# Sums of squares of attention keys in a four-stage fused kernel: one column of ones per block against a row of 512 per head, two heads side by side

## The chip, the cores and the metric

The kernel runs on one core of a Trainium2 chip. The core has TensorE (PE in the profile; PEld is its weight load), VectorE (DVE), ScalarE (ACT), GpSimd (POOL) and SyncE (SP, which here issues most DMAs), an SBUF of 128 partitions, and PSUM, to which TensorE writes. Each engine takes its instructions in the order in which the program gives them. The metric is device time in microseconds (us) of one launch, the median of several runs; lower is better.

## The reference

Four layers on x of 4 batches by 512 tokens by 512 channels, with a context of 4 by 512 by 256: a selective scan over the context, gated by the normed x; a mixture of 64 experts with 8 of them for each token; cross attention with 16 heads of 128; and a feed-forward with values rounded to integers. The change touches the third alone:

```python
def rmsnorm(x, g, eps=EPS):
    var = jnp.mean(jnp.square(x), axis=-1, keepdims=True)
    return x * jax.lax.rsqrt(var + eps) * g
...
q = (hidden_states @ Wq).reshape(B, Sq, H, D)
k = (encoder_hidden_states @ Wk).reshape(B, Skv, H, D)
v = (encoder_hidden_states @ Wv).reshape(B, Skv, H, D)
q = rmsnorm(q, gq)
k = rmsnorm(k, gk)
scores = jnp.einsum('bqhd,bkhd->bhqk', q, k) * scale
attn = jax.nn.softmax(scores, axis=-1)
out = jnp.einsum('bhqk,bkhd->bqhd', attn, v)
out = out.reshape(B, Sq, H * D)
return out @ Wo
...
x = x + _L0_xattn_ref(ctx_1024, _layernorm(x, axis=-1), ...)
x = x + _L0_ffn_ref(_layernorm(x, axis=-1), ...)
x = x + _L1_xattn_ref(_layernorm(x, axis=-1), ctx_1024, ...)
x = x + _L1_ffn_ref(_layernorm(x, axis=-1), ...)
```

There are 4 x 16 = 64 pairs of a batch and a head; each has 512 keys of 128 values, and for each key the sum of the squares of its 128 values is wanted.

## The kernel before

Keys depend on the context only, not on the layers before the attention. So the kernel makes them ahead of time, spread as small tasks through the earlier stages, and keeps them in DRAM until the attention reads them. Times below are from the start of the profiled span.

**The keys' tasks.** The class Keys (lines 1194 to 1258) has four steps for one pair of a batch and a head, and every stage calls them where it has room:

- task (line 1223): TensorE multiplies the 128 weight columns of the head by the context, four instructions into a PSUM bank pk of 128 (values of a key) by 512 (keys).
- evict: ACT writes two copies from PSUM to SBUF: k_sq, the squares (line 1232), and k_kT, the keys times gk (line 1233). SP sends k_kT, 256 KB, to DRAM (k_dram, line 1234).
- squares (line 1243): the sums over the 128 partitions. Each block of 128 columns of k_sq is the weight of a matmul with one column of ones; the result is one column of a PSUM tile kpss of 128 by 4. A float32 matmul is two instructions in the profile, so a head has 8.
- take (line 1255): ACT divides by 128 and adds the epsilon into k_ms, 128 by 4, and SP writes it to four columns of ms_dram (line 1257).

k_sq is free again when TensorE has read it. Which SBUF tile it lives in is asked of the stage (row), as is the PSUM bank (psum).

**Where they run.** 64 heads are split so: in the scan 5 each of batches 1, 2 and 3, and all 16 of batch 0 in its last quarter; in the route 17; in the attention the last 16, heads 8 to 15 of batches 2 and 3 (KEYS_LATE).

- The scan (0 to about 509) works through 128 steps q; in each, POOL multiplies dBu (line 494), ACT makes dA by exponentials, VectorE scans and TensorE turns the products. A plan gives each head its q: task at the end of step q, evict at the start of q+2, squares at its end, take at the start of q+3. The heads of batches 1 to 3 start at steps 14, 22, 24, 26 and 30 of a batch's 32, those of batch 0 at every second step.
- The route (to about 635) chooses each token's experts. A loop over 16 blocks of 128 tokens, two in a turn, normalises (g_xn), turns (g_pt), multiplies by the gate (g_plT), takes exponentials and masks (g_z, stored in z_dram; POOL presets the tile by memsets). From its second turn on it makes one head in each turn, with squares and take of the head of the turn before between the next blocks' turns and the logits. After the loop a plan by due times places the steps: mapping, ranks and codes, then lists of tokens (ol, ob, ot and the product plist). A helper two_keys gives the task of one head, then squares and take of the head before, then the eviction of the new one. It is placed twice ahead of the lists and once at the end, and four more heads lie among the lists.
- The experts (to about 1293): 64 in order, each with gathers by POOL, turns of the gathered rows (pt, line 1307, copied by ACT or VectorE to xT), pg (line 1343), and po (lines 1367, 1377). Small tasks are placed between the experts, as many per expert as the count of tasks demands. The last are key_norms (lines 1605 to 1626): load the means of squares of 48 heads from ms_dram as 128 by 192, take the inverse square roots (ACT's root, then VectorE), and then turn them by TensorE in two steps (kpt, krows), so that each row has 128 keys, and store the rows in r_dram, from which the attention reads rows broadcast over partitions.
- The attention (to the end) starts with 8 of the late heads, one every 2.6 us of its plan (some_keys: task, squares of the head before, evict, take of the head before), while POOL gathers the experts' results (yg) and adds them up. Then four windows of 14.5 us of plan each project the queries (pq) of a block of tokens, with two key heads in each. k_sq is a tile of the ring of two called planes, k_kT one of the ring of seven called oT; planes is afterwards filled by the attention's own transposes by DMA. The means of squares go directly into columns of an SBUF tile ms. last_norms (line 2346) takes the inverse roots in unit 16 of the steady loop, and last_keys (line 2349) turns and stores them in unit 24.

Of the kernel before, what the change touches and what calls it, by code (L numbers as in the profile page):

```python
# [17 lines left out]
F32 = mybir.dt.float32  # L18
# [12 lines left out]
P = 128  # L31
# [4 lines left out]
EPS = 1e-5  # L36
# [206 lines left out]
def ssm_phase(ctx, cm, x_all, w, kv, router_stats):  # L243
# [347 lines left out]
    def ahead_ends(b, s):  # L591
# [11 lines left out]
        if s == 23:  # L603
# [6 lines left out]
    keys = Keys(cm, w, kv, cm.k_small, lambda n: pool[1].tile([P, S], F32, name=f"k_{n}"),  # L610
                lambda shape, name: ps.tile(shape, F32, name=name, tag=banks[name]),
                lambda b: (st[b]["ctx"], 0))
# [5 lines left out]
    def key_task(b, h, bank):  # L618
        banks.update(pk=bank, kpss="pv")
        keys.task(b, h)  # L620
# [119 lines left out]
def moe_phase(ctx, cm, x_all, w, kv, dr, router_stats, out):  # L740
# [20 lines left out]
    with ExitStack() as es:  # L761
# [3 lines left out]
        keys = Keys(cm, w, kv, cm.k_small, None, None, None)  # L765
# [29 lines left out]
def route(ctx, cm, x_all, w, dr, router_stats, r, more, late, keys, ex):  # L795
# [91 lines left out]
    def key_row(n):  # L887
        if n == "sq":
            return cp.tile([P, S], F32, name="k_sq")
# [300 lines left out]
    plan.run()  # L1190
    assert not left


class Keys:
# [6 lines left out]
    def __init__(self, cm, w, kv, small, row, psum, ctx, direct=None):  # L1201


        self.cm, self.nc, self.w, self.kv = cm, cm.nc, w, kv
        self.small, self.row, self.psum, self.ctx, self.direct = small, row, psum, ctx, direct
        self.wk = {}
        self.pk = self.sq = self.pss = None
# [19 lines left out]
    def evict(self):  # L1227
# [3 lines left out]
        sq, kT = self.row("sq"), self.row("kT")  # L1231
# [3 lines left out]
        self.pk, self.sq = None, (b * H + h, sq)  # L1235

    def squares(self):
        if self.sq is None:
            return
        i, sq = self.sq  # L1240
        pss = self.psum([P, self.KB], "kpss")
        for j in range(self.KB):
            self.nc.tensor.matmul(pss[:, j:j + 1], sq[:, j * P:(j + 1) * P], self.cm.ones[:, 0:1],  # L1243
                                  start=True, stop=True)
        self.sq, self.pss = None, (i, pss)

    def take(self):
        if self.pss is None:
            return
        i, pss = self.pss  # L1250
        if self.direct is None:
            ms = self.small.tile([P, self.KB], F32, name="k_ms")
        else:
            ms, self.direct = self.direct[:, 0:self.KB], self.direct[:, self.KB:]
        self.nc.scalar.activation(ms, pss, AF.Copy, bias=EPS, scale=1.0 / HD)
        if self.direct is None:
            self.nc.sync.dma_start(self.kv["ms"][:, i * self.KB:(i + 1) * self.KB], ms)
# [218 lines left out]

def slot_tasks(cm, dr, kv, r, pool, ps):
# [119 lines left out]
    cols = []  # L1597
    for k in range(B * H + 1):
        if k < B * H and k not in late:
            if not cols or cols[-1][1] < k * KB:  # L1600
# [952 lines left out]
```

## The time and the profile before

| | us |
|---|---|
| median of 3 runs | 2471.33 |
| lowest, highest run | 2467.07, 2478.49 |
| the profiled execution, its own time | 2469.94 |
| its span in the trace | 2468.2 |

The mean TensorE clock of the profiled execution was 0.979 of full. The groups of the instructions that the change touches:

| group | count | busy us | mean ns of one |
|---|---|---|---|
| PE kpss (line 1243), 128x1 out | 512 | 66.8 | 251 |
| PEld kpss, 128x128 weights | 512 | 65.1 | 196 |
| ACT k_ms from kpss, 128x4 | 64 | 10.8 | 169 |
| ms_dram from k_ms, issue by SP, 2.0 KB each | 48 | | 320 |
| k_dram from k_kT, 256.0 KB each | 64 | | |

A group's busy time counts overlapping instructions once, its mean is the time of one as it was recorded; matmuls are pipelined, so what a series takes on TensorE is read from where the next one starts. In a timeline each line has start, duration, engine, line, operation, output and inputs, shapes and count; a bracket at its end says how long the engine was idle before it and what ended that. In a chain each piece is what the next one waited for. A row of stretches has for each engine its busy time in a stretch of the span, and then the granted clock, the busy share of the DMA engines and GB/s.

### The profile page before, as it was taken

What the parts mean: (1) busy time and instruction counts of PE and PEld (TensorE: products, weight loads), DVE (VectorE), ACT (ScalarE), POOL (GpSimd) and SP (SyncE); (2) the same over time, 40 slices, a digit from 0 to 9 for tenths busy, and PEclk for the clock granted to TensorE, in tenths of its full rate; (3) what the DMA queues carried; (4) which work ended last, traced back from release to release, by engine and by line L of the source; (5) the groups of instructions that cost most, each with busy time, mean ns of one, the idle gap of its engine ahead of it and who ended that gap; (6) DMA issues with size and microseconds to landing.
All of it is one profiled execution on the core that took longest, in us unless ns stands there. A gap on an engine that the chain in (4) does not pass through costs nothing. (4 is left out here: it accounts for less than half of the span.)

```text
span 2468.2 us, 29177 instructions
## 1 busy us (share of the span) xinstructions
PE 2330.2 (94%) x8819; PEld 1268.0 (51%) x8819; DVE 1590.2 (64%) x2872; ACT 1414.0 (57%) x2647; POOL 1332.1 (54%) x1314
## 2 busy tenths in 40 slices
PE   5989899988899999999998999999999999999998
PEld 2555555655555656666664444444444444444444
DVE  6999998956244434444324477667776778666655
ACT  6777777755333333344433466667666666667654
POOL 7999999940444434544426356356644655333323
PEclk8999998998999999999998999999999999999999
DMA  5362727343689868899976478678866887566530
GB/s 213 94 231 90 246 86 246 103 163 110 211 254 294 265 226 276 272 285 346 303 220 214 152 190 219 155 186 196 188 160 159 190 191 175 136 156 150 132 78 26
DMA packets 479892, 468.01 MB, mean 190 GB/s; under 512 B 313247, under 2 KB 354287, under 8 KB 475632
## 3 DMA queue, kind: packets, MB, share of 16 engines
q1 hardware_dynamic: 434686, 305.77, 46.3%
q0 software_dynamic: 42992, 160.13, 20.0%
q8 instruction: 72, 1.18, 0.2%
q14 instruction: 92, 0.75, 0.1%
q10 hardware_dynamic: 2050, 0.18, 0.1%
HBM read 316.11 MB, written 79.82 MB: 160 GB/s over the span
## 5 line engine op out<-in xcount | busy, mean ns | idle before, releaser
L1343 PE MATMUL pg<-xT,wg 128*128 128x284 f32 (+12 forms) x1536 | 389.4, 399 | 2.3 <-ACT xT L1310 1.3
L2027 POOL COPY planes<-e 128x512 int16<-128x512 int16 x174 | 119.2, 685 | 397.5 <-DVE e L2008 215.5
L1999 DVE TENSOR_REDUCE mx<-psc 128x1 f32<-128x512 f32 x256 | 176.3, 689 | 243.0 <-PE psc L1996 240.2
L1343 PEld LDWEIGHTS pg<-xT,wg 128*128 128x128 f32 x1536 | 280.4, 191 | 93.1 <-issue 40.2
L494 POOL TENSOR_TENSOR dBu<-bb,du 128x1024 f32<-128x1024 f32 x128 | 304.8, 2411 | 6.6 <-DVE dA L519 5.5
L2002 ACT ACTIVATE e<-psc,mx 128x512 f32<-128x512 f32 x256 | 176.3, 689 | 148.6 <-DVE mx L1999 77.6
L1996 PE MATMUL psc<-kT,qT 128*128 128x512 f32 x512 | 260.0, 594 | 0.0
L2068 PE MATMUL po<-eT,v 128*128 128x512 f32 x512 | 236.8, 605 | 13.5 <-ACT eT L2062 10.7
L1264 POOL DMA_INDIRECT xg<-xn_dram,tok x168 | 176.4, 1050 | 123.9 <-PE pt L1307 59.9
L1962 PE MATMUL pq<-Wq,xnT 128*128 128x512 f32 x512 | 231.8, 595 | 4.8 <-ACT xnT L1918 3.9
L2077 PE MATMUL px<-Wo,oT 128*128 128x512 f32 x512 | 231.2, 595 | 2.3 <-DVE qn L1980 2.3
L505 ACT ACTIVATE dA<-delta,negA 128x512 f32<-128x512 f32 x256 | 176.3, 694 | 50.9 <-DVE hc L520 37.3
L519 DVE TENSOR_TENSOR_SCAN dA<-dA,dBu 128x1024 f32<-128x1024 f32 x80 | 185.7, 2322 | 15.2 <-ACT dA L505 7.9
L1264 POOL DMA_INDIRECT wd<-down,widx x64 | 61.9, 967 | 225.1 <-PE po L1377 212.0
L2068 PEld LDWEIGHTS po<-eT,v 128*128 128x128 f32 x512 | 92.0, 189 | 150.7 <-issue 91.8
L1962 PEld LDWEIGHTS pq<-Wq,xnT 128*128 128x128 f32 x512 | 96.2, 190 | 129.8 <-issue 110.6
L2077 PEld LDWEIGHTS px<-Wo,oT 128*128 128x128 f32 x512 | 95.1, 190 | 125.5 <-issue 105.5
L525 PEld LDWEIGHTS yT<-ident,hc 128*128 128x128 f32 x1024 | 118.6, 143 | 74.5 <-issue 42.4
L1883 POOL DMA_INDIRECT yg<-y_dram,pos x108 | 118.1, 1094 | 59.0 <-issue 50.1
L1388 ACT COPY yo<-po 128x512 f32<-128x512 f32 (+3 forms) x64 | 37.5, 586 | 195.3 <-PE po L1377 150.5
L525 PE MATMUL yT<-ident,hc 128*128 128x128 f32 x1024 | 132.0, 276 | 17.6 <-DVE x_all L560 9.9
L1388 DVE COPY yo<-po 128x512 f32<-128x512 f32 x68 | 46.9, 691 | 151.3 <-PE po L1377 151.3
(380 smaller groups left out, 4696.6 us busy)
## 6 DMA issues: line engine op xcount, KB each, us to landing
y_dram<-yo SPq DMA_DIRECT2D x110, 256.0 KB
bb<-bc_dram SPq DMA_DIRECT2D x16, 1024.0 KB
cb<-bc_dram SPq DMA_DIRECT2D x16, 1024.0 KB
v_dram<-v SPq DMA_DIRECT2D x64, 256.0 KB
k_dram<-k_kT SPq DMA_DIRECT2D x64, 256.0 KB
kT<-k_dram SPq DMA_DIRECT2D x64, 256.0 KB
rk<-r_dram SPq DMA_DIRECT2D x64, 256.0 KB
v<-v_dram SPq DMA_DIRECT2D x64, 256.0 KB
```

Of the source, the lines that this page charges most:

```text
L494: nc.gpsimd.tensor_tensor(dBus[q], st[b]["bb"][i // 2][:, j:j + 2, :], st[b]["du"][c].unsqueeze(1).to_broadcast([P, 2, S]), ALU.mult)
L505: nc.scalar.activation(dAs[q][:, j, :], st[b]["delta"][c], AF.Exp, scale=negA[:, c, n:n + 1])
L519: nc.vector.tensor_tensor_scan(*flat, 0.0, ALU.mult, ALU.add)
L525: nc.tensor.matmul(yT[:, lc, :], t[:, lc * P:(lc + 1) * P], cm.ident, is_transpose=True, start=first and lc == 0, stop=last, skip_group_ch ...
L1264: nc.gpsimd.indirect_dma_start(out=t[0:n, :], out_offset=None, in_=table, in_offset=bass.IndirectOffsetOnAxis(ap=index, axis=0))
L1343: nc.tensor.matmul(pg[:, 0:n], s["wg"][:, c, m * P:(m + 1) * P], s["xT"][:, c, 0:n], start=c == 0, stop=c == NC - 1)
L1962: nc.tensor.matmul(pq.rearrange("p h d -> p (h d)"), xnTs[b * NC + i][:, c, :], s["Wq"][:, c, :], start=c == 0, stop=c == NC - 1)
L1996: nc.tensor.matmul(pscore, st[b, g]["qT"][:, h, i * P:(i + 1) * P], ks[n], start=True, stop=True)
L1999: nc.vector.tensor_reduce(mx, pscore, AX.X, ALU.max, negate=True)
L2002: nc.scalar.activation(e, pscore, AF.Exp, bias=mx, accum_out=tot)
L2068: nc.tensor.matmul(po, v[:, kc, :], eT[:, kc, :], start=kc == 0, stop=kc == KB - 1)
L2077: nc.tensor.matmul(px, oTs[j * HG + h][:, i * P:(i + 1) * P], st[b, g]["Wo"][:, h, :], start=h == 0, stop=h == HG - 1)
```

## The change

The sums of squares come out as a row. The weights are now 64 columns of ones, and the moving operand is the whole k_sq of 512 columns, so that a head is one matmul (two instructions) whose 64 output rows are all the same sum. Two heads go one after the other, the first into the PSUM partitions 0 to 63, the second into 64 to 127. squares does nothing until two heads have been evicted (n=2), but the heads of batches 1 to 3 in the scan go alone (n=1), and a last head that is left over can be forced (last=True), which the end of the route does.

take makes one copy from PSUM of 128 (or 64) by 512, in place over the k_sq of the first head of the pair, and one DMA of a 2 KB row for each head into ms_dram, which is now 64 by 512. A k_sq tile is therefore held until that row has left. The tiles of a pair: in the scan's last quarter two pairs in the former taps tile; in the route one tile with two halves; in the attention two tiles of the ring oT, from which k_kT is taken as well, in place of planes.

With rows in DRAM the norms need no turn: any layout of 128 partitions will do for the inverse root, so they are loaded flat, and stored flat (move_norms). key_norms has three steps instead of four. The late heads of the attention go through ms_dram as well, and the three steps of last_norms (load, root, store) are in the units 16, 20 and 24.

```diff
@@ -607,15 +607,29 @@
 
 
     banks = {}
-    keys = Keys(cm, w, kv, cm.k_small, lambda n: pool[1].tile([P, S], F32, name=f"k_{n}"),
+    spare = []
+
+    def key_row(n):
+        if n == "kT" or keys.n == 1:
+            t = pool[1].tile([P, S], F32, name=f"k_{n}")
+            return t if n == "kT" else [t]
+        if not spare:
+            t = cp.tile([P, NC, DC, P], F32, name="k_sqs", tag="taps")
+            spare.extend([t[:, i].rearrange("p j s -> p (j s)") for i in range(k, k + 2)]
+                         for k in (0, 2))
+        spare.append(spare.pop(0))
+        return list(spare[-1])
+
+    keys = Keys(cm, w, kv, key_row,
                 lambda shape, name: ps.tile(shape, F32, name=name, tag=banks[name]),
-                lambda b: (st[b]["ctx"], 0))
+                lambda b: (st[b]["ctx"], 0), n=1)
     key_plan = {}
 
     def key_at(q, ends, f, *a):
         key_plan.setdefault((q, ends), []).append((f, a))
 
     def key_task(b, h, bank):
+        keys.n = 1 if b > 0 else 2
         banks.update(pk=bank, kpss="pv")
         keys.task(b, h)
 
@@ -762,7 +776,7 @@
         more = es.enter_context(tc.tile_pool(name="b_more", bufs=1))
         r["tok"] = more.tile([P, 3, E], I32, name="tok")
         r["widx"] = more.tile([P, E], I32, name="widx")
-        keys = Keys(cm, w, kv, cm.k_small, None, None, None)
+        keys = Keys(cm, w, kv, None, None, None)
         with tc.tile_pool(name="e_w", bufs=4) as wp:
             ex = Experts(cm, w, dr, y_dram, r, wp)
             route(cm, x_all, w, dr, router_stats, r, more, late, keys, ex)
@@ -886,7 +900,8 @@
 
     def key_row(n):
         if n == "sq":
-            return cp.tile([P, S], F32, name="k_sq")
+            t = cp.tile([P, 2, S], F32, name="k_sq")
+            return [t[:, 0], t[:, 1]]
         if not kTs:
             t = late.tile([P, 2, S], F32, name="k_kT", tag="hq")
             kTs.extend([t[:, 0], t[:, 1]])
@@ -1188,6 +1203,8 @@
     for f in (some_key, keys.evict, two_keys, key_ends):
         plan.at(U + 1.8 * NT + 5, f)
     plan.run()
+    keys.squares(last=True)
+    keys.take()
     assert not left
 
 
@@ -1198,13 +1215,16 @@
     KC = CTX // P
     KB = S // P
 
-    def __init__(self, cm, w, kv, small, row, psum, ctx, direct=None):
+    HALF = P // 2
+
+    def __init__(self, cm, w, kv, row, psum, ctx, n=2):
 
 
         self.cm, self.nc, self.w, self.kv = cm, cm.nc, w, kv
-        self.small, self.row, self.psum, self.ctx, self.direct = small, row, psum, ctx, direct
+        self.row, self.psum, self.ctx, self.n = row, psum, ctx, n
         self.wk = {}
-        self.pk = self.sq = self.pss = None
+        self.pk = self.pss = None
+        self.sqs, self.free = [], []
 
     def load(self, h0, h1, pool, tag, queue=None):
 
@@ -1228,33 +1248,35 @@
         if self.pk is None:
             return
         b, h, pk = self.pk
-        sq, kT = self.row("sq"), self.row("kT")
+        if not self.free:
+            self.free = self.row("sq")
+        sq, kT = self.free.pop(0), self.row("kT")
         self.nc.scalar.activation(sq, pk, AF.Square)
         self.nc.scalar.activation(kT, pk, AF.Copy, scale=self.cm.gkq)
         self.nc.sync.dma_start(self.kv["k"][b, h], kT)
-        self.pk, self.sq = None, (b * H + h, sq)
-
-    def squares(self):
-        if self.sq is None:
+        self.pk = None
+        self.sqs.append((b * H + h, sq))
+
+    def squares(self, last=False):
+
+        if len(self.sqs) < self.n and not (last and self.sqs):
             return
-        i, sq = self.sq
-        pss = self.psum([P, self.KB], "kpss")
-        for j in range(self.KB):
-            self.nc.tensor.matmul(pss[:, j:j + 1], sq[:, j * P:(j + 1) * P], self.cm.ones[:, 0:1],
-                                  start=True, stop=True)
-        self.sq, self.pss = None, (i, pss)
+        pss = self.psum([P, S], "kpss")
+        for j, (_, sq) in enumerate(self.sqs):
+            self.nc.tensor.matmul(pss[j * self.HALF:(j + 1) * self.HALF, :],
+                                  self.cm.ones[:, 0:self.HALF], sq, start=True, stop=True)
+        self.pss, self.sqs, self.free = (self.sqs, pss), [], []
 
     def take(self):
         if self.pss is None:
             return
-        i, pss = self.pss
-        if self.direct is None:
-            ms = self.small.tile([P, self.KB], F32, name="k_ms")
-        else:
-            ms, self.direct = self.direct[:, 0:self.KB], self.direct[:, self.KB:]
-        self.nc.scalar.activation(ms, pss, AF.Copy, bias=EPS, scale=1.0 / HD)
-        if self.direct is None:
-            self.nc.sync.dma_start(self.kv["ms"][:, i * self.KB:(i + 1) * self.KB], ms)
+        sqs, pss = self.pss
+        ms = sqs[0][1]
+        at = slice(0, len(sqs) * self.HALF)
+        self.nc.scalar.activation(ms[at], pss[at], AF.Copy, bias=EPS, scale=1.0 / HD)
+        for j, (i, _) in enumerate(sqs):
+            self.nc.sync.dma_start(self.kv["ms"][i:i + 1, :],
+                                   ms[j * self.HALF:j * self.HALF + 1, :])
         self.pss = None
 
 
@@ -1474,6 +1496,18 @@
     return ctx
 
 
+def move_norms(nc, kv, rk, runs, load):
+
+    KB, at = S // P, 0
+    for k0, k1 in runs:
+        flat = (kv["ms"][k0:k1, :].rearrange("k s -> (k s)") if load else
+                kv["r"][k0 * KB:k1 * KB, :].rearrange("n p -> (n p)"))
+        flat = flat.rearrange("(p m) -> p m", p=P)
+        part = rk[:, at:at + (k1 - k0) * KB]
+        nc.sync.dma_start(*((part, flat) if load else (flat, part)))
+        at += (k1 - k0) * KB
+
+
 def slot_tasks(cm, dr, kv, r, pool, ps):
 
 
@@ -1594,43 +1628,27 @@
 
     KB = S // P
     late = {b * H + h for b, h in KEYS_LATE}
-    cols = []
-    for k in range(B * H + 1):
-        if k < B * H and k not in late:
-            if not cols or cols[-1][1] < k * KB:
-                cols.append([k * KB, k * KB])
-            cols[-1][1] += KB
-    n = sum(c1 - c0 for c0, c1 in cols)
+    runs = []
+    for k in range(B * H):
+        if k not in late:
+            if not runs or runs[-1][1] < k:
+                runs.append([k, k])
+            runs[-1][1] += 1
+    n = sum(k1 - k0 for k0, k1 in runs) * KB
 
     def key_norms(step):
         if step == 0:
             c["rk"] = pool.tile([P, n], F32, name="krk")
-            at = 0
-            for c0, c1 in cols:
-                nc.sync.dma_start(c["rk"][:, at:at + c1 - c0], kv["ms"][:, c0:c1])
-                at += c1 - c0
         elif step == 1:
             rsqrt(nc, pool, c["rk"], c["rk"], "k")
             return lambda: None
-        else:
-            a0, a1 = (step - 2) * P, min((step - 1) * P, n)
-            pt = ps.tile([P, P], F32, name="kpt", tag="pt")
-            pe.transpose(pt[0:a1 - a0, :], c["rk"][:, a0:a1], cm.ident)
-            rows = pool.tile([P, P], F32, name="krows")
-            act.copy(rows[0:a1 - a0, :], pt[0:a1 - a0, :])
-            at = 0
-            for c0, c1 in cols:
-                lo, hi = max(at, a0), min(at + c1 - c0, a1)
-                if lo < hi:
-                    nc.sync.dma_start(kv["r"][c0 + lo - at:c0 + hi - at, :],
-                                      rows[lo - a0:hi - a0, :])
-                at += c1 - c0
+        move_norms(nc, kv, c["rk"], runs, step == 0)
 
     calls = [(load,), (rooms,), (many,), (row, "limit"), (row, "first"), (weigh, 0), (weigh, 1)]
     calls += [(inside, n) for n in range(4)] + [(tops, q) for q in range(NT // NC)]
     calls += [(remap, q) for q in range(NT // NC)]
     calls += [(weight, k, i) for k in range(TOPK) for i in range(3)] + [(finish,)]
-    norms = [(key_norms, i) for i in range(2 + -(-n // P))]
+    norms = [(key_norms, i) for i in range(3)]
     return [[lambda f=f, a=a: f(*a) for f, *a in part] for part in (calls, norms)]
 
 
@@ -2260,11 +2278,16 @@
 
     n_ms = len(KEYS_LATE) * KB
     ms = pool[1].tile([P, n_ms], F32, name="k_ms")
+    late_runs = []
+    for b, h in KEYS_LATE:
+        if not late_runs or late_runs[-1][1] < b * H + h:
+            late_runs.append([b * H + h, b * H + h])
+        late_runs[-1][1] += 1
 
     def key_row(n):
 
         if n == "sq":
-            return pool[2].tile([P, S], F32, name="k_sq", tag="planes")
+            return [pool[7].tile([P, S], F32, name="k_sq", tag="oT") for _ in range(2)]
         return pool[7].tile([P, S], F32, name=f"k_{n}", tag="oT")
 
     def key_bank(shape, name):
@@ -2272,10 +2295,8 @@
             return pav.tile(shape, F32, name=name, tag="po")
         return psc.tile(shape, F32, name=name, tag="psc")
 
-    keys = Keys(cm, w, kv, small, key_row, key_bank,
-                lambda b: (ctx_k[b], 0), direct=ms)
+    keys = Keys(cm, w, kv, key_row, key_bank, lambda b: (ctx_k[b], 0))
     keys.wk = wk_k
-    first = KEYS_LATE[0][1]
 
     steps = []
 
@@ -2343,18 +2364,11 @@
     for n in range(3):
         later(FRONT + (0, 2.5, 3.2)[n] * WINDOW + 9, norm_k, n, nc.vector)
 
-    def last_norms():
-        rsqrt(nc, small, ms, ms, "late")
-
-    def last_keys():
-        pr = ptr.tile([n_ms, P], F32, name="pkr", tag="pt")
-        nc.tensor.transpose(pr, ms, cm.ident)
-        rows = pool[1].tile([n_ms, P], F32, name="k_rows", tag="xn_d")
-        nc.scalar.copy(rows, pr)
-        for b in (2, 3):
-            at = (b * H + first) * KB
-            nc.sync.dma_start(kv["r"][at:at + n_ms // 2, :],
-                              rows[(b - 2) * n_ms // 2:(b - 1) * n_ms // 2, :])
+    def last_norms(step):
+        if step == 1:
+            rsqrt(nc, small, ms, ms, "late")
+        else:
+            move_norms(nc, kv, ms, late_runs, step == 0)
 
 
     for *_, f, a in sorted(steps, key=lambda x: x[:2]):
@@ -2363,8 +2377,8 @@
     load_q(2)
     load_o(0, 0)
     load_kv(3)
-    put(back, KB * 3 + 4, last_norms)
-    put(back, KB * 5 + 4, last_keys)
+    for step in range(3):
+        put(back, KB * (3 + step) + 4, last_norms, step)
 
 
     for u in range(KB, len(heads) * KB + 2):
@@ -2484,7 +2498,7 @@
     dp = ctx.enter_context(tc.tile_pool(name="kv", bufs=1, space=DRAM))
     kv = dict(v=dp.tile([B, H // HG, P, S // P, HG * HD], F32, name="v_dram"),
               k=dp.tile([B, H, HD, S], F32, name="k_dram"),
-              ms=dp.tile([P, B * H * (S // P)], F32, name="ms_dram"),
+              ms=dp.tile([B * H, S], F32, name="ms_dram"),
               r=dp.tile([B * H * (S // P), P], F32, name="r_dram"))
     dr = dict(xn=dp.tile([B * S, DM], F32, name="xn_dram"),
               z=dp.tile([NT, P, 3, Gate.W], F32, name="z_dram"))
```

## The prediction

> **What bounds the kernel now.** I read the page first (engines, slices, chain), then the stretches stage by stage, then the timeline around each place where squares of keys are made, and last the chain through the start of the attention.
>
> The page: TensorE is busy 94% of the span, and the chain that ended last names its lines first. The squares (L1243) stand there with 0%, which is a share of the whole span only.
>
> ```profile
> PE 2330.2 (94%) x8819; PEld 1268.0 (51%) x8819; DVE 1590.2 (64%) x2872; ACT 1414.0 (57%) x2647; POOL 1332.1 (54%) x1314
> PE po L2068 8%; PE pq L1962 7%; PE psc L1996 6%; PE px L2077 6%; PE pf L2181 2%; DMA turned<-planes 2%; PE ph L2146 1%; DVE mx L1999 1%; PE pk L1223 1%; PE pet L2061 1%; ACT e L2002 1%; ACT Th L2111 1%; DVE e L2008 0%; PE kpss L1243 0%; DVE x_all L1891 0%
> ```
>
> Stretches (start:end, length, then busy us of PE, PEld, DVE, ACT, POOL, clock, DMA share): the scan (85 to 505) has PE, DVE and POOL all above 90%, POOL highest; the route (505 to 640) has no full engine, so its time is latency from one engine to the next; the experts (700 to 1276) are TensorE's, 571 of 576.
>
> ```profile
> 85.00:200.00 115.00, 104.61 (x462) 61.67 (x461) 109.60 (x79) 86.39 (x141) 110.14 (x57) 0.97 0.51 167
> 505.00:580.00 75.00, 63.44 (x319) 38.00 (x317) 36.23 (x178) 42.92 (x94) 20.91 (x80) 0.93 0.43 149
> 580.00:640.00 60.00, 49.10 (x290) 32.71 (x286) 33.77 (x75) 29.45 (x46) 12.06 (x12) 0.84 0.36 117
> 700.00:1276.00 576.00, 571.06 (x2548) 369.36 (x2545) 245.43 (x473) 219.22 (x465) 261.85 (x257) 1.00 0.90 281
> ```
>
> Timeline of the route: the squares stand between a wait for ACT and the logits, on TensorE's path; two heads later an f16 copy (ot) follows k_sq and k_kT on ACT, and VectorE waits for what it feeds.
>
> ```profile
> 545.72 1.05 PE L1243 MATMUL kpss<-ones,k_sq 128*128 128x1 f32 x8 [0.40 <-ACT k_kT L1233]
> 546.70 1.94 PE L204 MATMUL g_plT<-g_xT,gwT 128*64 128x256 f32 x8
> ...
> 556.28 0.10 POOL L221 MEMSET g_z<- 128x4 f32 x1 [0.46 <-DMA z_dram<-g_z]
> ...
> 590.93 0.17 ACT L1255 ACTIVATE k_ms<-kpss 128x4 f32<-128x4 f32 x1 [1.26 <-PE kpss L1243]
> 591.00 0.59 ACT L1232 ACTIVATE k_sq<-pk 128x512 f32<-128x512 f32 x1
> 592.05 1.16 ACT L1033 ACTIVATE ot<-ol,tok 128x1024 f16<-128x1024 f16 x1
> 594.65 0.96 DVE L1026 TENSOR_TENSOR ob<-slot_col,col 128x1536 f16<-128x1536 int16 x1 [2.86 <-PE plist L1041]
> 635.38 1.07 PE L1307 MATMUL pt<-ident,xg 128*128 128x128 f32 x8
> ```
>
> Chain through the attention's start (start, us, what): key projections and squares alternate and end in the first pq; later two squares stand between pq's.
>
> ```profile
> 1310.85 2.55 PE kpss L1243 x8
> 1318.01 1.87 PE kpss L1243 x8
> 1333.23 3.45 PE pq L1962 x8
> 1375.24 0.79 PE kpss L1243 x8
> 1390.21 0.79 PE kpss L1243 x8
> ```
>
> **Prices.** One head before: 8 instructions, 0.79 us in the chain when warm. One head as a row of 512 is one f32 matmul, two instructions; px, pq and pk in the chain take 0.43 per instruction (pq x8 3.45), so 0.86. A pair is 0.86 if its two column halves run together and 1.72 if one after the other. The nearest row is the expert's pair of half-array matmuls (po L1377, 64-row tiles): four instructions occupy TensorE from 1206.80 to 1207.86, 1.06. I take 1.1 a pair against 1.58 for two heads before. ACT's k_ms was 0.17; a 128x512 copy from PSUM is 0.59 (yo L1388, v L482), so +0.42 a take, +0.25 a pair.
>
> The new wait: squares' tile is written in place by the take and is free only when its row has landed in DRAM; before, TensorE's read freed it. Price of one return: semaphore records give 1.4 us after issue for the ms store of 626.89 and 5.9 for that of 635.75, behind other transfers; the z store, issued at 553.13, released POOL at 555.68, 2.5. I take 2 in the quiet route, 3.4 in the attention's start (DMA share 0.74 in 1310 to 1360); 1.4 and 5.9 are the bounds.
>
> The Trainium skill, TensorEngine Tiling (Array Packing), Key Properties, says that changing the tiling mode drains TensorE, which speaks against the change: every pair is set between full-array matmuls. The 1.06 above has both switches in it and is 0.2 over one full matmul of 0.86; were a drain as long as a whole matmul, the pair would be 1.72 and the sum some 6 us higher. No column pair is in this trace.
>
> **Step by step.**
>
> 1. Scan, 31 heads. 15 alone: TensorE +0.07 each, +1.0; 16 as 8 pairs: 8 × (1.1 − 1.58) = −3.8. ACT: 23 × 0.59 − 31 × 0.17 = +8.3. ACT is busy 86 of 115 us and POOL 110, so this hides under dBu and hc on POOL; without that cover +8.3 at most, −3.8 at best. For the heads of batches 1 to 3 the single sq tile is refilled one step (450 us for 128 dBu, 3.5) after the take; behind a late square on ACT stands dA, for which VectorE's scan waits, with buffers between. Taken: 0. But the last pair has no cover: the cast of ident and g_xn queue behind its take (508.53, g_xn 508.80): +0.42 on ACT and +0.3 on TensorE (1.1 − 0.79), **+0.7** (0 to 1.4).
>
> 2. Route loop. Seven heads had their squares in six turns of 7.0 us and once behind the loop (0.98 start to next, after a wait of 0.40). Now three turns have a pair and three none; nothing is left behind the loop. In a turn without, g_plT may start when g_pt ends (545.33) rather than at 546.70: 1.37. But the exps (549.91, 556.92) also wait for POOL's memset, that for the z store of the turn before: exps 549.91 to memset's end 556.34 is 6.43, so a turn gets no shorter than that and gains 0.58. Three × −0.58, behind the loop −0.98, pairs +0.1 each; the longer take falls into ACT's 0.5 us wait for g_plT. **−2.4**; −5.1 if z doesn't hold (3 × 1.37 + 0.98), +0.7 with serial halves and takes on the path.
>
> 3. Two heads ahead of the lists (586 to 594). The second head's k_sq needs the pair's tile: squares 589.95 + 1.1, take to 591.7, store back at 593.7 by the 2 us, k_sq; ot follows 1.05 later at 594.75 instead of 592.05: **+2.7**, since VectorE and TensorE wait for ot's plist already (2.86). With 1.4: +2.1; with 5.9: +6.6. The same wait at 575 to 583 falls into an ACT that idles 6.96 us ahead of 588.49: nothing; if that cover were gone, as here. Token lists: two longer takes, +0.42 each, one of which plist waits for: **+0.5** (0 to 1).
>
> 4. Route's end. Seventeen heads are odd: pair 14/15 is squared, taken (632.76 + 1.1 + 0.6), stored; head 16's k_sq waits, is squared alone, and only behind that, in TensorE's order, stands the first expert's pt. Store back at 636.5, k_sq 0.6, squares 0.9: pt at 638 instead of 635.38, +2.6. The copy behind pt started only at 638.47, by a wait that the trace leaves unnamed, so part is slack: **+2.0** (0.2 with all of it slack, 6.6 with a return of 5.9). The experts, full on TensorE, keep this shift.
>
> 5. Norms among the experts. Two turns by TensorE (0.44 in all) go, and ACT's second krows copy with its 5.39 us wait for the r store; that expert's turn took 9.05 against 8.4 to 8.5 of its neighbours. **−0.9** (0 to −1). Loads and stores stay three or four, with flat rows; their queue is full either way. The square root stays.
>
> 6. Attention's start, TensorE then POOL. On the chain to pq at 1333.23 the squares are 8.9 us (0.79, 0.79, 2.55, 1.87, 1.03, 0.79, 1.05); four pairs at 1.1 to 2.2 (half clock) save about 4. Against it: kT of heads 3, 5 and 7 takes a slot of the ring of seven that an in-place row leaves one turn (2.6) earlier; issue 0.3 + 3.4 − 2.6 = 1.1, three times 3.3. **−0.7**; −4 with quick returns, 3 × (0.3 + 5.9 − 2.6) − 4 = +6.8 with slow ones. POOL, idle 10.4 us ahead of qms, passes it on.
>
> 7. Windows to 1400: the squares at 1375.24 and 1390.21 leave the chain, the pairs go to 1382 and 1397, where TensorE waits 0.5 for qn: **−1.6** (−1.6 to 0). The late norms: eight more pairs of row stores, loads and stores at three places, the turn of 0.27 and the copy of 0.26 gone, all long before the first use: 0.
>
> Sum: 0.7 − 2.4 + 2.7 + 0.5 + 2.0 − 0.9 − 0.7 − 1.6 = +0.3. The profiled execution took 2469.94 us (span 2468.2, 1.7 around it), 1.4 under the median of the runs; +0.3 on the median 2471.33 gives 2471.6, rounded to 2472.
>
> **Rivals.**
> - Rows come back late (slower). One mechanism: the in-place tile held until its store lands, at three places on the path. At 5.9: 6.6 + 6.6 + 6.8 with the other terms unchanged (0.7 − 2.4 + 0.5 − 0.9 − 1.6 = −3.7) is +16.3: 2488. It decides over 0.5% from about 5.2 on. For it: the store of 635.75, in the very place. Against: that of 626.89.
> - Gains without givebacks (faster). Returns of 1.4 and z not binding: 0.4 − 5.1 + 2.1 + 0 + 0.2 − 0.9 − 4 − 1.6 = −8.9: 2462. For it: TensorE is the chain at the attention's start. Against: POOL gathers yg from 1340 on without a break, so 4 us of that may hide.
> - The halves don't overlap: each pair 1.72, +0.6 at some ten pairs on the path: +6, 2478. For it: none is in the trace to deny it. Against: 1.06 for two row tiles.
> - The scan loses its cover, ACT's 8.3 showing whole: 2480. Against: ACT's 25% idle.
>
> **How the numbers follow.** Forecast 0.45, late rows 0.22, faster 0.18, serial halves 0.08, scan 0.07. About 0.5%, 12.4 us, is what a measurement of this kernel tells from no change: 2459 to 2484. Late rows mostly pass 2484, the others seldom; of the faster case a good half passes 2459 only if TensorE's relief also reaches the scan's −3.8. So faster 0.15, same 0.58, slower 0.27. The range takes both neighbours in: 2459 to 2488.
>
> **What would show it.** Squares: four instructions a pair, ending within 1.1. Route turns alternating near 6.4 and 7.1. ACT waiting for an ms store ahead of k_sq near 592 and 635; the first ot near 594.7; the first pt near 638. The r wait of 5.4 gone. pq's first at about the same distance from the attention's start. The forecast is wrong if pairs take 1.7, if stalls name the ms store for over 5 us each, or if the stretches up to 505 change length at all.

## The result, and the profile after

The changed kernel takes 2481.2 us (median of 22 runs, 2468.09 to 2492.32); the kernel before, in the same comparison, 2470.24 (22 runs, 2460.98 to 2485.11). The ratio is 1.0046, with a 95% interval of 1.0033 to 1.0059: 11 us slower. The profiled execution took 2485.54 us, with a span of 2483.8 and a clock of 0.976.

The first lines of the page of the changed kernel, busy time and chain by line:

```profile
PE 2315.9 (93%) x8432; PEld 1215.7 (49%) x8432; DVE 1592.9 (64%) x2872; ACT 1427.6 (57%) x2620; POOL 1329.0 (54%) x1314
PE po L2086 8%; PE pq L1980 7%; PE psc L2014 6%; PE px L2095 6%; PE pf L2199 2%; DMA turned<-planes 2%; PE ph L2164 2%; DVE mx L2017 1%; ACT e L2020 1%; PE pet L2079 1%; DMA k_dram<-k_kT 1%; ACT Th L2129 1%; PE pk L1243 1%; DVE e L2026 0%; DVE qn L1998 0%
```

TensorE is 14 us less busy than before, as the change meant, and the span is 16 us longer. The stretches of the same kernel say where to look:

```profile
85.00:200.00 115.00, 103.65 (x422) 56.30 (x421) 107.80 (x78) 86.86 (x139) 109.15 (x57) 0.97 0.51 166
580.00:640.00 60.00, 39.23 (x195) 21.39 (x194) 28.35 (x51) 31.68 (x42) 13.87 (x14) 0.82 0.39 129
700.00:1276.00 576.00, 558.27 (x2455) 360.91 (x2454) 239.37 (x461) 211.25 (x447) 255.95 (x252) 0.98 0.88 271
```

The scan is as it was. The experts (third row), in which the change touches four small steps, have lost: TensorE works 558 of 576 us there, before 571, at a clock of 0.98 for 1.00. To place the loss, the table takes the start of one instruction at the border of each stage from the traces and lists the distances in us. Each value is one profiled execution; the kernels with 84 tasks belong to the experiments below.

| from, to | before (2 profiles) | changed (3 profiles) | changed, 84 tasks (2) | predicted |
|---|---|---|---|---|
| first dBu, last dBu (scan) | 467.7, 467.6 | 468.2, 466.1, 468.7 | 468.8, 468.7 | 0 |
| last dBu, first g_xn | 9.7, 9.7 | 9.6, 9.5, 9.5 | 9.5, 9.5 | +0.7 |
| first g_xn, last g_plT (loop) | 60.5, 60.7 | 53.9, 53.7, 56.5 | 54.5, 54.4 | -1.4 |
| last g_plT, first ot | 22.8, 22.8 | 23.3, 23.2, 23.2 | 23.4, 23.3 | +1.7 |
| first ot, tok | 37.3, 37.3 | 37.7, 39.3, 38.0 | 36.5, 36.8 | +0.5 |
| tok, first pg (route's end) | 11.4, 10.3 | 14.6, 15.1, 14.7 | 14.7, 14.8 | +2.0 |
| first pg, last pg (experts) | 646.4, 652.1 | 667.4, 658.8, 668.5 | 645.2, 645.1 | -0.9 |
| last pg, first px | 156.4, 153.1 | 150.0, 148.3, 149.1 | 145.4, 149.0 | -2.3 |
| first px, px no. 100 | 178.1, 178.1 | 182.4, 182.4, 182.4 | 182.4, 182.2 | 0 |
| px no. 100, last px | 809.2, 808.1 | 807.4, 802.7, 809.6 | 805.8, 804.5 | 0 |

(The 0.98 saved behind the loop is counted with the fourth row.) The loop gains 6, the experts lose 16, the route's end loses 4, and the attention gains 6 at its start and loses 4 later.

The timeline of the experts at the norms, changed kernel, ScalarE and then TensorE:

```profile
1220.35 0.59 ACT L1410 COPY yo<-po 120x512 f32<-120x512 f32 x1 [2.05 <-PE po L1399]
1227.51 1.28 ACT L97 ACT_TABLE_LOAD   x1 [6.58 <-DMA krk<-ms_dram]
...
1233.69 3.57 PE L1365 MATMUL pg<-xT,wg 128*128 128x240 f32 x8 [5.15 <-ACT xT L1352]
```

ScalarE stands 6.58 us for the load of the means of squares (krk). Behind it, in its order, are the copies that bring the next expert's xT, and TensorE waits 5.15 for one of them. What comes behind the wait is slow as well: these eight instructions of pg take 3.57, the eight of the expert before (at 1220.20) took 1.89, and the granted clock is 0.50 from 1233.6 to 1237. Before, that load was issued at 1201.20 and the root's table load began at 1208.61, an expert later, with nothing to wait for. In the changed kernel the load was issued at 1221.91, directly ahead of the root.

The reason is a number that no line of the diff names. The small tasks are handed out by `done < (i - 1) * many / QUOTA`, i being the expert's turn and many the count of tasks. With key_norms at three steps instead of four, many falls from 84 to 83. Worked out from that line, and from the rule in the same loop that a task with a second half (the root counts as one) ends its turn: load, root and turns were in the turns 53, 54 and 55, and are now load and root in 54, store in 55; 21 other tasks move by one turn as well (the expectations below say 20).

A second thing in the same stretch, at another place:

```profile
1132.99 0.76 ACT L1352 COPY xT<-xt 128x512 int16<-128x512 int16 x1 [7.93 <-DMA xt<-xh]
1133.81 1.65 PE L1365 MATMUL pg<-xT,wg 128*128 128x256 f32 x3 [5.55 <-ACT xT L1352]
```

A transpose by DMA was issued at 1120.04, and the copy that waits for it starts 12.9 us later.

### The profile page after: what moved, and what is told of

It is laid out like the page before. It is cut to its first block, busy times and chain, and to the rows that moved or that the text cites. A ratio compares the mean times of both kernels' runs of the same rounds, so it can differ in the third digit from the quotient of the medians.

```text
span 2483.8 us, 28362 instructions
## 1 busy us (share of the span) xinstructions
PE 2315.9 (93%) x8432; PEld 1215.7 (49%) x8432; DVE 1592.9 (64%) x2872; ACT 1427.6 (57%) x2620; POOL 1329.0 (54%) x1314
## 5 line engine op out<-in xcount | busy, mean ns | idle before, releaser
L1365 PE MATMUL pg<-xT,wg 128*128 128x284 f32 (+12 forms) x1536 | 395.8, 404 | 13.3 <-ACT xT L1352 11.9
L519 DVE TENSOR_TENSOR_SCAN dA<-dA,dBu 128x1024 f32<-128x1024 f32 x80 | 188.4, 2355 | 14.4 <-issue 6.1
```

The lines of the kernel that those rows point to most:

```text
L519: nc.vector.tensor_tensor_scan(*flat, 0.0, ALU.mult, ALU.add)
L1365: nc.tensor.matmul(pg[:, 0:n], s["wg"][:, c, m * P:(m + 1) * P], s["xT"][:, c, 0:n], start=c == 0, stop=c == NC - 1)
```

## The experiments

**The changed kernel and the one before, once more.** No edit; for the scatter of the stages.

> The changed kernel once more. If the loss is laid down by the order of the instructions (theory: key_norms' load and root now fall into the same expert, and ACT waits for the load), the wait of ACT's root for krk of 6 to 7 us is there again, and the stretch of the experts is again 15 us or more longer than before's. If it was chance (rival: the late DMA transposes that expert turns wait for), the stretch of the experts differs from the first profile by 5 us or more. Time 2475 to 2487.

> The kernel before once more, for a second profile of its stages. Theory: no wait of the root for krk, the experts' stretch within 3 us of the first profile's. Rival (chance): it moves by 5 us or more. Time 2465 to 2476.

Measured: the changed kernel 2479.23, ratio 1.0072 (1.0045 to 1.0099); the kernel before 2468.85, ratio 1.0005 (0.9986 to 1.0024). The root waited again, 7.6 us, in the changed kernel alone. Aligned with the kernel of 84 tasks below, instruction by instruction, both profiles of the changed kernel lose the same amounts at the same places of the experts: 1.0 near 820, 3.3 between 900 and 940, 1.1 near 1060 (5.4 in sum), and 8.2 at the norms. One part was chance: the late transposes near 1120 cost 8.7 in the first profile and nothing in the second, which is why the stretch is 667 in one and 659 in the other. Before's stretch also moved by 5.7; so both theories had a share.

**The pace alone, both ways.** The diff is that of the changed kernel; in the kernel before it is `- 1`.

```diff
-        many = len(tasks)
+        many = len(tasks) + 1
```

> The changed kernel with the count of small tasks that paces them raised by one, to the 84 of before, so that load, root and store of the norms fall into three experts in a row again (53, 54, 55) and 20 tasks return to the experts where before had them. Theory: the root's wait for krk goes (6 to 7 us), the experts' stretch falls by 7 us at least against the changed kernel's, by up to 21 if the other late turns came of the pace too; time 2465 to 2474, faster than the changed kernel by 7 to 15. Rival (chance): only the wait at the root goes, the total falls by under 4.

> The kernel before with the same count lowered by one, to 83: its load and root fall into one expert (54), its two turns into 55 and 56; nothing else is changed. Theory: the root waits for krk by 4 to 7 us and the kernel takes 5 to 12 us more than before: 2475 to 2482. Rival (the loss comes of rows and pairs): no difference over 3 us.

> The changed kernel with 84 tasks once more, beside the two others on one chip. Theory (the pace makes the whole loss): faster than before by 0.1 to 0.5% and faster than the changed kernel by 10 to 18 us. Rival (the first comparison was luck): within 5 us of the changed kernel.

Measured: the changed kernel with 84 tasks took 2460.85, ratio 0.9985 (0.9963 to 1.0007), beside 2479.23 for the changed kernel on that chip; again on another chip 2461.26, ratio 0.9958 (0.994 to 0.9977), beside 2486.25. The kernel before with 83 tasks took 2479.39, ratio 1.0059 (1.0036 to 1.0082), 13 us over the 2466.21 of before in that round, where 5 to 12 were expected. So the loss goes with the count and comes with it, without any square being touched: this is shown from both sides. ScalarE at the root, in the kernel before with 83 tasks, and then in the changed kernel with 84:

```profile
1216.12 0.59 ACT L1388 COPY yo<-po 120x512 f32<-120x512 f32 x1 [2.04 <-PE po L1377]
1224.07 1.28 ACT L97 ACT_TABLE_LOAD   x1 [7.37 <-DMA krk<-ms_dram]
```

```profile
1206.47 0.59 ACT L1410 COPY yo<-po 120x512 f32<-120x512 f32 x1 [2.05 <-PE po L1399]
1207.07 1.28 ACT L97 ACT_TABLE_LOAD   x1
```

The wait is in the one that has the old squares and the new count, and missing in the one that has the new squares and the old count. The gains over the changed kernel, 18 and 25 us, were more than the 7 to 15 and 10 to 18 that were expected. Against the kernel before, the one with 84 tasks is faster in the second comparison; in the first no difference is shown.

**How the pace's price is made up.**

```diff
         tasks += slots[len(halves):] + halves[len(slots):] + norms
+        tasks[-4], tasks[-3] = tasks[-3], tasks[-4]
```

> The changed kernel with its own pace (83 tasks), but the norms' load exchanged with the task before it, so that it stands an expert ahead of the root again; the other tasks stay where the change put them. If load and root in one expert are the whole of the pace's price, the time is that of the kernel with 84 tasks, 2458 to 2466. If the price is shared with the 20 other tasks that moved, only the wait of 6.6 to 7.6 us goes: 2469 to 2475. If that wait is hidden, 2477 to 2483.

Measured: 2478.06, ratio 1.0008 (0.9987 to 1.0028). As a time this is the last case; but the kernel before took 2476.13 in this round, 6 to 10 us more than in the two earlier ones, so the ratio is the better measure, and by it the middle case holds: below the changed kernel's 1.0046 (1.0033 to 1.0059), and not shown to differ from before. The profile says it plainly: no step at the norms any more, but the 5.4 us near 820, 900 to 940 and 1060 are all there, and transposes are late near 1120 (7.5 us). So in the changed kernel the root's wait is 8.2 of the loss (with the slow instructions behind it), the three other places 5.4, and the late transposes the rest. These transposes cost 6 to 9 in four of five profiles with 83 tasks, and nothing in eight of nine with 84; the ninth, the kernel with single heads below, lost 11.5. That the pace brings them about more often is likely by these counts; which other transfer holds them up was not tried.

What stands at the three places can be read from the traces, here of the changed kernel, and then pw in the kernel with 84 tasks:

```profile
814.25 0.35 PE L1837 MATMUL pm<-wone,ones 128*128 128x1 f32 x2 [0.73 <-DVE wone L1833]
932.44 1.79 PE L1593 MATMUL pw<-map,s_wT 64*128 64x64 f32 x8 [2.11 <-ACT s_wT L1588]
1062.75 0.35 PE L1837 MATMUL pm<-wone,ones 128*128 128x1 f32 x2 [0.90 <-DVE wone L1833]
```

```profile
907.27 1.10 PE L1593 MATMUL pw<-map,s_wT 64*128 64x64 f32 x8 [2.06 <-ACT s_wT L1588]
```

- pm, the second half of a task that takes a mean, waits 0.7 and 0.9 for VectorE in all five profiles with 83 tasks and does not wait in the nine with 84. With 83, another VectorE task, of 1.2 us, has moved into its turn and stands ahead of it at both places. These two steps, 2.1 in sum, go with the count.
- pw waits 2.1 us for ScalarE twice in every profile, whatever the count; with 83 tasks the second wait stands two experts later (at 932.44 instead of 907.27). What differs is the clock behind the waits. By the clock records of the traces, TensorE ran at half speed between 885 and 945 for 10.2 us in all four profiles of the changed kernel with 83 tasks, for 3.4 or 6.8 in the nine with 84 (3.4 in the one that the steps are measured against), and not at all in the kernel before with 83, which lost nothing there. At half speed half of the time is lost: of 10.2 less 3.4 that is 3.4, and the step is 3.3. That this step follows from the count alone is therefore not shown.

**The wait for the in-place row.** This edit and the next two are made to the changed kernel with 84 tasks.

```diff
-        ms = sqs[0][1]
+        ms = self.out() if self.out else sqs[0][1]
...
+    keys.out = lambda: cp.tile([P, S], F32, name="k_out")
```

> The changed kernel with 84 tasks, and in the route a tile of its own for the take, so that no k_sq waits for an ms row to land. Theory (the wait for the row stands on the path at the lists and at the route's end): the stretch from the first ot back to the loop's end shortens by 2.0 to 2.8, and the first pg comes 2 to 3 us earlier than the wait lets it: 4 to 5 us in all against the kernel with 84 tasks. Rival: the lists and the first expert wait for something else as long (xg, plist): under 1.5.

Measured: 2453.63 (6 runs), ratio 0.9912 (0.9888 to 0.9936). The kernel with 84 tasks alone did not run in this round, so what the tile adds is read from the stretches. Last g_plT to first ot went from 23.4 to 20.6, as expected. ScalarE at the lists, in the changed kernel and then with the tile of its own:

```profile
582.49 0.60 ACT L1276 ACTIVATE k_sq<-kpss 128x512 f32<-128x512 f32 x1 [1.58 <-PE kpss L1266]
585.86 0.60 ACT L1254 ACTIVATE k_sq<-pk 128x512 f32<-128x512 f32 x1 [2.77 <-DMA ms_dram<-k_sq]
586.35 0.68 ACT L1255 ACTIVATE k_kT<-pk,gkq 128x512 f32<-128x512 f32 x1
586.92 2.18 ACT L1048 ACTIVATE ot<-ol,tok 128x1024 f16<-128x1024 f16 x2
```

```profile
581.15 0.60 ACT L1277 ACTIVATE k_out<-kpss 128x512 f32<-128x512 f32 x1 [1.58 <-PE kpss L1267]
581.64 0.59 ACT L1255 ACTIVATE k_sq<-pk 128x512 f32<-128x512 f32 x1
582.12 0.69 ACT L1256 ACTIVATE k_kT<-pk,gkq 128x512 f32<-128x512 f32 x1
582.69 2.19 ACT L1049 ACTIVATE ot<-ol,tok 128x1024 f16<-128x1024 f16 x2
```

The 2.77 between take and k_sq is gone, and the ot with it is earlier. At the route's end the rival held: tok to first pg fell from 14.7 to 13.6 only (14.4 in the kernel with all mends), because the first xT then waits for the gathered rows:

```profile
631.09 0.59 ACT L1333 COPY xT<-pt 128x512 f32<-128x512 f32 x1 [2.73 <-DMA xg<-xn_dram,tok]
```

Something was given back ahead of it: last dBu to first g_xn took 11.0 instead of 9.5, in all three kernels that have the larger pool of the route. Why, was not tried.

**Pairs or single rows.**

```diff
+    keys.n = 1
     keys.out = lambda: cp.tile([P, S], F32, name="k_out")
```

> As the kernel with a tile of its own for the take, but the route squares every head alone (n=1): a row of 512 each, no pairs. If the loop's gain came of the turns that have no squares, the loop (first g_xn to last g_plT) goes back from 54 to 59 or more, since each of six turns has 0.9 us of squares and a wait for k_kT again, and 1 us comes back behind the loop. If it came of the form (512 columns against eight narrow instructions), it stays at 54 to 55.

Measured: 2464.1, ratio 0.9957 (0.9936 to 0.9978), in the same round as the one above: 10 us slower. The loop took 57.3; with pairs and the same tile it took 52.5 here and 54.6 in the kernel with all mends, so the loss is 2.7 to 4.8, less than expected. From first g_xn to first pg it is 5.3 (128.8 against 123.6); where the rest of the 10 arises can't be read from the profile, which is of an execution of 2480.45, far above the median. The starts of g_plT say what a turn costs, first with single heads, then in the changed kernel with pairs (kpss of the pair between the second and the third):

```profile
539.15 1.89 PE L204 MATMUL g_plT<-g_xT,gwT 128*64 128x256 f32 x8
546.04 1.89 PE L204 MATMUL g_plT<-g_xT,gwT 128*64 128x256 f32 x8
552.93 1.89 PE L204 MATMUL g_plT<-g_xT,gwT 128*64 128x256 f32 x8
```

```profile
537.30 1.89 PE L204 MATMUL g_plT<-g_xT,gwT 128*64 128x256 f32 x8
542.81 1.94 PE L204 MATMUL g_plT<-g_xT,gwT 128*64 128x256 f32 x8
548.78 1.08 PE L1266 MATMUL kpss<-k_sq,ones 128*64 128x512 f32 x4 [0.34 <-ACT k_kT L1255]
549.69 1.89 PE L204 MATMUL g_plT<-g_xT,gwT 128*64 128x256 f32 x8
555.21 1.94 PE L204 MATMUL g_plT<-g_xT,gwT 128*64 128x256 f32 x8
```

Single: 6.89 each. Pairs: 5.51 without squares, 6.88 with. The row form alone takes 0.13 off a turn of 7.02; leaving the squares out takes 1.5. A pair, two heads, has four instructions, and the next matmul starts 0.91 after its first, as it does behind the two of a single head (0.91 too): the two column halves run side by side.

**The late norms' place.**

```diff
-        put(back, KB * (3 + step) + 4, last_norms, step)
+        put(back, KB * (2 + step) + 4, last_norms, step)
```

> The changed kernel with 84 tasks, and the late heads' norms at units 12, 16 and 20 of the attention's loop: the root at 16, where it was before. If the root's table loads ahead of the softmax cost what the stretch from the first px to the hundredth shows (182.4 against 178.1), that stretch returns to 178 to 179, and the stretch ahead of it grows by at most 2.5: 2 to 4 us in all. Rival: the root costs the same wherever it stands, the sum of both stretches stays within 1 us.

Measured: 2460.61, ratio 0.9946 (0.9924 to 0.9967). First px to px no. 100 returned to 178.0, in both kernels with the root at unit 16, against 182.2 to 182.4 in all profiles of the change with the root at 20. The stretch ahead of it, from first psc to first px, grew by 2.4 (95.1 to 97.5); but two profiles of the changed kernel itself differ by 3.1 there (94.4 and 97.5), so this growth is not clear of the scatter. The changed kernel, root at unit 20:

```profile
1460.85 1.28 ACT L97 ACT_TABLE_LOAD   x1
1462.14 0.26 ACT L97 ACTIVATE rs_t_late<-k_ms 128x64 f32<-128x64 f32 x1
1464.68 1.28 ACT L2020 ACT_TABLE_LOAD   x1 [2.29 <-DVE mx L2017]
...
1468.39 1.96 PE L2086 MATMUL po<-eT,v 128*128 128x512 f32 x2 [2.56 <-ACT eT L2080]
```

Two table loads stand among the softmax's exponentials, and TensorE waits 2.56 for the transposed e behind them. At unit 16 it waited 1.21 for the same.

**The turns' tile.** The kernel before, each krows copy with a tile of its own.

```diff
-            rows = pool.tile([P, P], F32, name="krows")
+            rows = pool.tile([P, P], F32, name=f"krows{step}")
```

> The kernel before with a tile of its own for each of the two krows copies, so that the second doesn't wait for the first one's store (5.4 and 7.3 us in two profiles). If that wait is what the conversion without turns gains, the step at 1220 in the experts' stretch falls by 1 to 4.6 us, and nothing else changes; the time is 0 to 5 us below before's. If the turns themselves were the price, nothing falls.

Measured: 2470.06, ratio 0.9979 (0.9963 to 0.9996). Against the kernel with 84 tasks, the two profiles of the kernel before lose 1.1 and 4.6 us at the norms, this one 0.2, with both turns by TensorE still in it. So what the conversion without turns gains is the wait for the store, not the turns.

**All mends together, and the changed kernel a third time.** The diffs of 84 tasks, own tile and unit 16.

> All three edits together: 84 tasks, a tile of its own for the take in the route, the late root at unit 16. If they add up (2 to 3 us from the own tile at the lists, about as much from the root at 16), it is 3 to 8 us faster than the kernel with 84 tasks alone on the same chip and at least 0.6% faster than before. If one of them is hidden by another, within 2 us of the kernel with 84 tasks.

> The changed kernel a third time, on the same chip as its mended versions: 0.4 to 0.8% above before. Its experts' stretch shows again the three steps against the kernel with 84 tasks, near 820, 900 to 940 and 1060, 5.4 us in sum, and the root's wait of 8; the late transposes near 1120 may or may not come.

Measured on one chip, where the kernel before took 2475.22: all three edits 2457.51, ratio 0.9937 (0.9913 to 0.996); 84 tasks alone 2461.26, ratio 0.9958 (0.994 to 0.9977); the changed kernel 2486.25, ratio 1.0048 (1.0024 to 1.0071). The intervals of the first two overlap, so that the own tile and unit 16 add to the count's mend is not shown by the times. All three steps of the changed kernel, the root's wait (7.6) and late transposes (9.2) were there.

So there are versions of this change that beat both kernels, by 0.6% in the last comparison; the count of tasks is the edit that they need.

## Why the prediction came out as it did

The forecast was 2472, hence no change, with a range of 2459 to 2488; the time was 2481, inside the range, and slower by less than the 0.5% that was to count. The range was right, the reasons behind it only in part: the loss stands where the prediction saw a gain, and was made up for in places where it saw little. That the time fell inside the range is in part luck: 16 lost among the experts and 4 at the route's end met 6 gained in the loop and 6 at the attention's start. With the count kept, the change was faster than before by 5 us (not clear of zero) and by 14.

- **Norms among the experts, -0.9: this is the step that failed.** It priced what each step does and said that loads and stores stay as they were. It did not ask into which expert each would fall. The stretch took 10 to 19 us longer than the mean of before (667.4, 658.8 and 668.5 against 646.4 and 652.1), and 14 to 23 longer than that of the same kernel with 84 tasks: 8.1 to 8.6 at the root, 5.4 at the three other places, and in two of the three profiles 9 of late transposes. The term itself has the right sign where the pace is kept: 1.1 and 4.6 in the two profiles of before.
- **Route loop, -2.4: mechanism right, size off.** 4.0 to 7.0 by the table for the loop alone, where 1.4 was put. The step that mis-sized it was the limit by z. Turns of 5.51 are shorter than the 6.43 that it held for a floor: the POOL memset presets a tile for a later turn, and the exps don't wait for the memset that stood just ahead of them. In the changed kernel the exps at 546.02 run ahead of the memset at 547.23. The other end given, 5.1 (3 x 1.37 and 0.98), was nearer.
- **Pairs, 1.1: right, somewhat high.** 0.91 in the route, 1.01 ahead of a pk at the attention's start in the kernel with 84 tasks. Serial halves, 1.72, are ruled out. Not every pair stands between full-array matmuls, as the prediction had it: g_plT, which follows in the route, has 64 columns of weights too.
- **Two heads ahead of the lists, +2.7: right.** The wait was 2.6 to 2.9, and taking it away gave 2.8. The row of the table rose by 0.5 only instead of 1.7, because what fell away behind the loop was 2.2 (20.6 with the tile of its own against 22.8) and not 0.98.
- **Route's end, +2.0: right in kind, too small.** 4.0 by the means of the table. k_sq waited 2.8 to 3.2 for the row. What was left out: TensorE, idle for 4.11 us, came back at half speed; the last head's squares took 1.90 to the next start instead of 0.86, and the first pt's eight instructions 1.97 instead of 1.07. And the next wait in line, for the gathered rows, stood 1 us behind.
- **The attention's start and its windows, -2.3: right in sign.** 153 to 156 became 148 to 150; 1.3 to 2.4 of that may be the late root, which left this stretch (95.1 against 97.5 and 94.3 against 95.6 from first psc to first px in the two pairs of kernels that differ by its unit), but this is not clear of the scatter. Of the three stalls that were priced at the oT ring, the trace of the changed kernel shows a kT waiting for k_dram and a pq for its weights, not an ms row (its third profile has one k_sq that waits 1.4 for such a row).
- **Late norms, 0: wrong.** It was costed at nothing since the first use is far off. It is the root's place on ScalarE that costs: 4.3 in one stretch, less the 1.3 to 2.4 that it may take in the one ahead.
- **The scan, 0, and its end, +0.7:** 0 within 1.5; the end gained 0.1 instead.
- **Late rows as the rival on the slower side:** waits of 1.8 to 3.6 in the route, not the 5.9 that it needed. The time came near to its side for another reason.

Left open: from px no. 100 on, the changed kernel's profiles (802.7 to 809.6, with either count) are up to 6 us shorter than before's (808.1 and 809.2) and once no shorter, with no touched line in that stretch; which transfer holds up the late transposes; and whether the half-speed time between 885 and 945 follows from the count.

## What to carry to other kernels

Where small tasks are handed out by their count, taking one away moves the others: work out the new order, and look which load now stands just ahead of its use. A cheaper step is worth what its neighbours lose or gain by its place, here the root's two table loads and the wait for a row in flight, rather than its own microseconds. A wait of TensorE can also cost more than its length: behind those of 2 us and more here, it often ran at half speed for 3.4 to 10.2 us. And before a chain of waits is taken for a floor, check that the instruction really waits for the one ahead of it, and not just follows it.

## What the runs showed of the hardware

- Matmuls in the two column halves overlap wholly: of the four float32 instructions of a pair (512 columns, two for each half) the second starts 0.01 us after the first, and g_plT, which has 64 columns of weights as well, starts 0.91 after it; in the kernel with single heads, two instructions in one half, it is 0.91 too.
- A change between 128 and 64 columns of weights costs 0.09 us: behind a float32 instruction of 512 columns the next starts after 0.42 to 0.43 where the columns stay (pk to pk, kpss to g_plT) and after 0.52 where they change, in either direction (pk to kpss, kpss to pk). The Trainium skill, TensorEngine Tiling (Array Packing), Key Properties, has the array drained at a change of tiling mode. If these changes are such, 0.09 is all that a drain took here, and not the whole matmul that the prediction allowed for.
- In the kernel before, no copy of a tile transposed by DMA waited for its transfer; the copies started 8.6 us after the issue in the median. In the changed kernel one copy started 12.9 us after the issue, having waited 7.93 for the transfer.
- TensorE at half speed after a wait: in the profile of the changed kernel the clock falls to 0.5 about the end of the 4.11 us of waiting at the route's end and stays there for 10.2 us; for 6.8 us at the 5.15 of the norms; and for 3.4 and 6.8 us at the two waits of pw (2.06 and 2.11). In the kernel before with 83 tasks it stays at 1.0 at the same two waits of pw.
